# Spacing the block chains of a fused four-layer graph network: transposes and weight products one stage further behind, last block's factors from two banks

## The chip, the cores and the metric

The kernel runs on one core of a Trainium2 chip. The metric is the device time of one execution in microseconds; before the change it is 2231.47 us (median of 3 runs, 2231.07 to 2232.33). The profile is one execution of the same kernel with a span of 2227.8 us.

A core has five engines with one instruction queue each: PE (TensorE, matrix products and transposes), DVE (VectorE), ACT (ScalarE), POOL (GpSimd) and SP (SyncE, which issues the loads). They meet through semaphores. PE writes into PSUM banks, from which DVE and ACT read.

## The reference, cut to what matters

Four graph layers over 4096 nodes with 128 features each, one dense 4096x4096 matrix `adj` (64 MB in float32), and after each layer a residual and a layer norm:

```python
# layer 0: signed attention;  layer 1: two Chebyshev convolutions with elu
x = _layernorm(x + _L0_gnn_ref(x, adj, adj, W, a))
x = _layernorm(x + _L1_gnn_ref(x, adj, W0, b0, W1, b1))
# layer 2: 4 heads of 32, dense attention with multiplicative adj
h_prime = (x @ weight.T).reshape(n, heads, f_out)
C = alpha_src[None, :, :] + alpha_dst[:, None, :]
tau = adj_t * exp(maximum(0.2 * C, C))
z = einsum('mnh,nhf->mhf', adj_t * tau / tau.sum(axis=1, keepdims=True), h_prime)
x = _layernorm(x + z + bias)
# layer 3: h @ W_self + (adj @ h / clip(adj.sum(1), 1)) @ W_neigh
x = _layernorm(x + _L3_gnn_ref(x, adj, W_self, W_neigh))
```

For layer 2 the kernel splits the exponential into factors of the source node (`es`, `cs`, and `hc`, the head's features times `cs`) and of the target node (`dv`, from which `D` is spread over the partitions), so that a weight is `max(D, es) * a`.

## The kernel before, in words

Nodes are taken in blocks of 512 (`IB`; 8 blocks, `NB`) and tiles of 128 (32 tiles, `NT`; four of them, `TB`, per block). Layer 1 ends in a product of the adjacency with `w`, block by block: 32 loop products (L1104) of 128x512 per block add up in one bank, `pp` (block 1 in `num`). When a block is done, its chain of small steps ends layer 1 for it and prepares layer 2:

- `block_end` (L741): DVE adds and applies the elu (L748 to L752, with ACT's L750 and L751) into `oT`; PE transposes it (L754); DVE adds it to `x` and takes the statistics (L756 to L763), ACT normalizes (L766); PE transposes `x` (L768); ACT copies the result to `xT` (L770), POOL adds a bias row (L772); then two halves of the weight product (L778, `W2S`), each followed by two exponentials on ACT (`cs` and `es`, L780 and L781) and two products on DVE (`hc`, L784).
- `block_targets` (L788): PE's product with `WD` (L792), an exponential and a split into three bf16 parts on ACT and DVE (L794 to L801).
- `targets` of the first two passes (L841): PE's product with `selD` (L851), copied to `D` by ACT (L854).

All PE steps of the chain, other than a second product of some `targets`, write one bank, `px` (pool `ps_x` with one buffer), so that each waits for the reader of the one before. In the trace the two kinds of transposes show as L137, the line of their helper.

Layer 2 itself is a row of passes over all 32 tiles (class `Pass`). One `step` (L857) makes the weights of one tile: DVE computes `tau` (L866, twice 128x1024) and the first 704 columns of `tau2` (L872), POOL the rest of it (L873, L874). `tau` comes in four buffers. `load` (L818) has ACT copy the adjacency tile to a PSUM bank `a` and sum it (L838); passes 0 and 1 share a tile, so there is a copy for every two steps. `product` (L883) has PE add `tau` to `den` and `tau2` to `num`, four matrix products of 32 rows each, called a row of products here.

The order on PE, DVE, ACT and POOL is written out by hand (`manual_schedule`): an instruction stands in its engine's queue in the order in which the Python code emits it. Chains are generators in the queue `chains`, and `one(chains)` takes the first of them to its next `yield`. So a `yield` is a turn: what follows is emitted behind the loop products of the next turn. For the first three blocks the turn comes after every two loop products; from block 3 on (`ib > 2`) steps of passes 0 and 1 are mixed in, and the turn comes after two or four loop products, twice for each segment of `cuts` (L1094), with a `products()` at each segment's end. A block's chain thus runs in the loop of the next block. The chain of the last block runs in the `while` loop of L1123, where `held` says that this chain is not done; there an iteration has two steps and two rounds of `one(chains)` or more, and no loop products of layer 1. The remaining passes of layer 2 and layer 3's product with the adjacency (L977) follow, mixed as well.

Of the kernel before, what the change touches and what calls it, by code (L numbers as in the profile page):

```python
# [11 lines left out]
F32 = mybir.dt.float32  # L12
BF16 = mybir.dt.bfloat16
I32 = mybir.dt.int32
AF = mybir.ActivationFunctionType
# [4 lines left out]
P = 128  # L20
IB = 512
TB = IB // P
# [11 lines left out]
def adj_resnorm_d4(ctx: ExitStack, tc: tile.TileContext, x_in, xT_in, adj, adjT, w0g, w0gT, a0, w1a, b1a,  # L34
# [7 lines left out]
    nc = tc.nc  # L42
    N, F = x_in.shape
    NT = N // P
    NB = N // IB
# [3 lines left out]
    H = att_src.shape[1]  # L49
    FO = F // H  # L50
# [31 lines left out]
    es = const.tile([P, NT, H], F32, name="es")  # L82
    cs = const.tile([P, NT, H], F32, name="cs")
# [49 lines left out]
    def transpose4(pool, name, src, order=lambda r: r):  # L133

        p = pool.tile([P, TB, P], F32, name=name)
        for k in range(TB):
            order(nc.tensor.transpose(p[:, k, :], src(k), ident))  # L137
        return p
# [486 lines left out]
    def network(usual):  # L625

        with ExitStack() as whole:
# [113 lines left out]
            def block_end(ib, p):  # L741

                blk = slice(ib * IB, (ib + 1) * IB)
                tb = slice(ib * TB, (ib + 1) * TB)
                oT = l2w.tile([P, IB], F32, name="oT", tag="z")
                rn = l2w.tile([P, 2, IB], F32, name="rn", tag="nd")
                r, n = rn[:, 0, :], rn[:, 1, :]
                nc.vector.tensor_add(oT, p, h0T[:, blk])  # L748
                nc.vector.tensor_scalar(n, oT, B1B, 0.0, op0=ALU.add, op1=ALU.min)
                nc.scalar.activation(n, n, AF.Exp)  # L750
                nc.scalar.activation(r, oT, AF.Relu, bias=B1B)  # L751
                nc.vector.scalar_tensor_tensor(oT, n, -1.0, r, op0=ALU.add, op1=ALU.add)  # L752
                yield
                q = transpose4(ps_x, "px", lambda k: oT[:, k * P:(k + 1) * P])  # L754
                yield
                nc.vector.tensor_add(x[:, tb, :], q, x[:, tb, :])  # L756
                for t in range(ib * TB, (ib + 1) * TB):
                    stats(x[:, t, :], t)
                s = small.tile([P, TB], F32, name="rstd")
                m = small.tile([P, TB], F32, name="mean")  # L760
                nc.scalar.activation(s, mv[:, tb, 1], AF.Sqrt, bias=eps)
                nc.vector.reciprocal(s, s)
                nc.vector.scalar_tensor_tensor(m, mv[:, tb, 0], -1.0, s, op0=ALU.mult, op1=ALU.mult)  # L763
                for k in range(TB):
                    r = x[:, ib * TB + k, :]
                    nc.scalar.activation(r, r, AF.Identity, bias=m[:, k:k + 1], scale=s[:, k:k + 1])  # L766
                yield
                q = transpose4(ps_x, "px", lambda k: x[:, ib * TB + k, :])  # L768
                yield
                nc.scalar.copy(xT[:, blk], q.rearrange("p k i -> p (k i)"))  # L770
                nc.scalar.activation(m[:, 0:1], m[:, 0:1], AF.Exp, scale=0.0)
                nc.gpsimd.tensor_tensor(x[:, tb, :], x[:, tb, :], B2R[:, None, :].to_broadcast([P, TB, F]), ALU.add)  # L772
                for half in range(2):
                    two = slice(ib * TB + 2 * half, ib * TB + 2 * half + 2)
                    pn = ps_x.tile([P, 2, F + H], F32, name="px")
                    for k in range(2):
                        t = ib * TB + 2 * half + k
                        nc.tensor.matmul(pn[:, k, :], xT[:, t * P:(t + 1) * P], W2S, start=True, stop=True)  # L778
                    yield
                    nc.scalar.activation(cs[:, two, :], pn[:, :, F:F + H], AF.Exp, scale=0.2)  # L780
                    nc.scalar.activation(es[:, two, :], pn[:, :, F:F + H], AF.Exp, scale=0.8)  # L781
                    for k in range(2):
                        t = ib * TB + 2 * half + k
                        nc.vector.tensor_mul(hc[:, t], pn[:, k, 0:F].rearrange("p (h f) -> p h f", f=FO),  # L784
                                             cs[:, t, :][:, :, None].to_broadcast([P, H, FO]))
                ended.append(ib)

            def block_targets(ib):  # L788

                blk = slice(ib * IB, (ib + 1) * IB)  # L790
                pd = ps_x.tile([96, IB], F32, name="px")
                nc.tensor.matmul(pd, WD, xT[:, blk], start=True, stop=True)  # L792
                yield
                nc.scalar.activation(pd, pd, AF.Exp, scale=-0.8)  # L794
                nc.scalar.copy(dv[:, blk], pd)
                yield
                nc.vector.tensor_sub(pd, pd, dv[:, blk])
                nc.scalar.copy(dv[32:64, blk], pd[32:64, :])
                nc.scalar.copy(dv[64:96, blk], pd[64:96, :])
                nc.vector.tensor_sub(pd[64:96, :], pd[64:96, :], dv[64:96, blk])  # L800
                nc.scalar.copy(dv[64:96, blk], pd[64:96, :])  # L801

            def weights(nt, head, den):
                return cs[:, nt, head:head + 1].to_broadcast([P, FO]) if den else hc[:, nt, head, :]

            class Pass:
# [50 lines left out]
                def step(self, nt, a, ap):  # L857

                    assert self.made == 4
                    tau = l2w.tile([P, 4, IB], F32, name="tau", bufs=4)  # L860
                    tau2 = l2w.tile([P, 4, IB], F32, name="tau2", bufs=4)
                    n = 2 if self.wide else 1
                    flat = lambda t: t.rearrange("p q i -> p (q i)")
                    for q in range(0, 4, n):
                        head = self.parts[q][0]
                        nc.vector.scalar_tensor_tensor(flat(tau[:, q:q + n]), flat(self.D[:, q:q + n]),  # L866
                                                       es[:, nt, head:head + 1], ap, op0=ALU.max, op1=ALU.mult)
                    if self.wide:
                        t, t2 = flat(tau), flat(tau2)

                        only = self is passes[1] and layer1_done
                        nc.vector.tensor_tensor(t2[:, 0:OWN], t[:, 0:OWN], (a if only else ap)[:, 0:OWN], ALU.mult)  # L872
                        nc.gpsimd.tensor_tensor(t2[:, OWN:WB], t[:, OWN:WB], a[:, OWN:WB], ALU.mult)  # L873
                        nc.gpsimd.tensor_tensor(t2[:, WB:2 * WB], t[:, WB:2 * WB], a, ALU.mult)  # L874
                    else:
                        own = OWN4 // 2
                        rep = lambda v, q: v[:, None, :].to_broadcast([P, q, v.shape[1]])
                        nc.vector.tensor_tensor(tau2[:, 0:2, 0:own], tau[:, 0:2, 0:own], rep(ap[:, 0:own], 2), ALU.mult)  # L878
                        nc.gpsimd.tensor_tensor(tau2[:, 0:2, own:IB], tau[:, 0:2, own:IB], rep(a[:, own:IB], 2), ALU.mult)  # L879
                        nc.gpsimd.tensor_tensor(tau2[:, 2:4, :], tau[:, 2:4, :], rep(a, 2), ALU.mult)  # L880
                    return tau, tau2
# [140 lines left out]
            with tc.manual_schedule(engines={mybir.EngineType.PE, mybir.EngineType.DVE, mybir.EngineType.Activation,  # L1022
# [100 lines left out]
                while todo:  # L1123
                    step()
                    if wait:
                        wait = bool(pieces) and not one(pieces)
                    held = NB - 1 not in ended
                    if not held:
                        load()
                    if todo[0] == (passes[1], NT - 1):  # L1130
                        while passes[2].made < 4:
                            one(chains)
                    one(chains)
                    if held:
                        load()
                    step()
                    if not pieces:
                        one(chains)
                    load()
                    products()  # L1140
                    one(chains)
                    credit = min(credit + (2.0 if todo and todo[0][0].wide else 3.4), 6.0) if pieces else 0.0
                    while credit >= 1.0 and pieces and not wait:
                        credit -= 1.0
                        wait = one(pieces)
# [48 lines left out]
```

## Time and profile before

| | |
|---|---|
| time | 2231.47 us (2231.07 to 2232.33, 3 runs) |
| span of the profile | 2227.8 us, 22992 instructions |
| PE | 2135.1 us busy (96%) |
| DVE | 1184.2 us (53%) |
| POOL | 857.6 us (38%) |
| ACT | 562.5 us (25%) |
| DMA | 528.18 MB, mean 237 GB/s |
| granted PE clock, mean | 0.988 |

Times in the profile are microseconds from the start of the span, unless marked ns. A row of the view in order of time gives the start, the duration, the engine, the line and operation, what is written and read, the number of instructions merged, and in brackets the idle time of the engine before it and what ended that. A float32 matrix product shows as two records. Ends on PE are modelled, so rows overlap a little; starts are what to subtract. A row of waits gives total us, times and the longest. A row of stretches gives the stretch and its length, then for each engine its busy us (and instructions), then PE's granted clock, the DMA share and GB/s.

### The profile page before, as it was taken

Reading aid. Unit: us, or ns where it says so; the run is one execution under the profiler, and the core shown is the slowest. Engines: PE = TensorE matmul, PEld = TensorE weight load, DVE = VectorE, ACT = ScalarE, POOL = GpSimd, SP = SyncE. Lnnn points to the kernel's source line nnn. Section 1 sums busy time; section 2 is a strip of 40 time slices with the busy share of each in tenths; the row PEclk is TensorE's granted clock in tenths of the full one; section 3 lists DMA queues with packets and bytes.
Section 4 is the critical chain, followed back from the end, with each engine's and each line's share of the span. In section 5 each row is a group of like instructions: output and inputs, shape, how many; then the busy total and the mean of one; then the engine's idle time right before and its main releaser. Section 6 shows DMA issues by size and latency. Waiting matters only on the chain. (4 is left out here: it accounts for less than half of the span.)

```text
span 2227.8 us, 22992 instructions
## 1 busy us (share of the span) xinstructions
PE 2135.1 (96%) x8644; PEld 847.9 (38%) x8644; DVE 1184.2 (53%) x1832; ACT 562.5 (25%) x1014; POOL 857.6 (38%) x539
## 2 busy tenths in 40 slices
PE   8999999999999999999999999978999899999997
PEld 4344454444444444444443333322222222233333
DVE  5655460000011110000016787789999999999995
ACT  6755010000000000000033223235333433332213
POOL 0000000000000000000004776688999899989980
PEclk9999999999999999999999999989999999999999
DMA  9886658888767768777867556524666566635554
GB/s 396 333 324 228 224 196 288 301 300 301 268 231 253 245 226 279 262 261 262 280 235 248 187 196 224 208 76 170 240 234 243 189 246 241 225 135 194 189 173 170
DMA packets 87145, 528.18 MB, mean 237 GB/s; under 512 B 9328, under 2 KB 15472, under 8 KB 25712
## 3 DMA queue, kind: packets, MB, share of 16 engines
q1 hardware_dynamic: 80288, 521.64, 66.6%
q10 hardware_dynamic: 6736, 4.98, 0.7%
q8 instruction: 70, 1.15, 0.2%
q14 instruction: 51, 0.42, 0.1%
HBM read 524.49 MB, written 2.10 MB: 236 GB/s over the span
## 5 line engine op out<-in xcount | busy, mean ns | idle before, releaser
L866 DVE SCALAR_TENSOR_TENSOR tau<-D,es,a 128x1024 f32<-128x1024 f32 (+1 forms) x640 | 647.0, 1061 | 52.5 <-ACT a L838 32.0
L874 POOL TENSOR_TENSOR tau<-tau,chunk 128x1024 f32<-128x1024 f32 x192 | 459.4, 2392 | 12.3 <-DVE tau L866 11.7
L772 POOL TENSOR_TENSOR x<-x,B2R 128x512 f32<-128x512 f32 x8 | 10.2, 1274 | 1148.0 <-PE px L137 1148.0
L890 PE MATMUL num<-tau,hc 128*32 128x512 f32 x2048 | 331.5, 612 | 13.2 <-POOL tau L874 6.7
L890 PE MATMUL den<-tau,cs 128*32 128x512 f32 x2048 | 336.0, 602 | 2.1 <-DVE tau L866 0.4
L977 PE MATMUL pp<-chunk,xT 128*128 128x512 f32 (+1 forms) x488 | 231.7, 604 | 0.0
L838 ACT ACTIVATE a<-chunk 128x1024 f32<-128x1024 f32 x160 | 164.3, 1027 | 249.9 <-DVE tau L872 193.4
L664 PE MATMUL pacc<-chunk,t 128*128 128x512 f32 x512 | 223.5, 592 | 0.0
L664 PE MATMUL pacc<-chunk,v 128*128 128x512 f32 x512 | 222.5, 592 | 0.0
L664 PE MATMUL pacc<-chunk,x 128*128 128x512 f32 x512 | 222.1, 592 | 0.0
L873 POOL TENSOR_TENSOR tau<-tau,chunk 128x320 f32<-128x320 f32 x192 | 168.0, 875 | 133.6 <-DVE tau L866 74.0
L1104 PE MATMUL pp<-chunk,w 128*128 128x512 f32 x448 | 203.5, 598 | 0.8 <-DVE oT L748 0.8
L379 PE MATMUL pacc<-chunk,hw 128*128 128x512 f32 x408 | 187.1, 603 | 1.1 <-DVE numT L407 1.1
L872 DVE TENSOR_TENSOR tau<-tau,a 128x704 f32<-128x704 f32 x186 | 163.6, 880 | 0.0
L880 POOL TENSOR_TENSOR tau<-tau,chunk 128x1024 f32<-128x1024 f32 x64 | 152.2, 2377 | 1.0
L890 PEld LDWEIGHTS num<-tau,hc 128*32 128x32 f32 x2048 | 61.2, 110 | 231.0 <-issue 125.5
L890 PEld LDWEIGHTS den<-tau,cs 128*32 128x32 f32 x2048 | 79.0, 111 | 173.7 <-issue 98.7
L664 PEld LDWEIGHTS pacc<-chunk,v 128*128 128x128 f32 x512 | 97.2, 190 | 122.0 <-issue 122.0
L664 PEld LDWEIGHTS pacc<-chunk,x 128*128 128x128 f32 x512 | 96.3, 190 | 115.8 <-issue 115.8
L664 PEld LDWEIGHTS pacc<-chunk,t 128*128 128x128 f32 x512 | 96.1, 190 | 115.3 <-issue 115.3
L977 PEld LDWEIGHTS pp<-chunk,xT 128*128 128x128 f32 x488 | 85.7, 190 | 128.6 <-issue 125.8
L711 DVE COPY w<-ptr 128x512 f32<-128x512 f32 x8 | 5.5, 692 | 241.5 <-PE ptr L137 241.5
(238 smaller groups left out, 1688.1 us busy)
## 6 DMA issues: line engine op xcount, KB each, us to landing
chunk<-in_adjT SPq DMA_DIRECT2D x386, 1024.0 KB, 4.9
chunk<-in_adj SPq DMA_DIRECT2D x80, 1024.0 KB, 5.0
chunk<-in_adj SPq DMA_DIRECT2D x32, 512.0 KB, 5.1
keep<-in_adjT SPq DMA_DIRECT2D x13, 1024.0 KB, 10.8
xT<-in_xT ACTq DMA_DIRECT2D x8, 256.0 KB, 6.5
out<-o ACTq DMA_DIRECT2D x7, 256.0 KB, 2.3
W1A<-in_w1a ACTq DMA_DIRECT2D x1, 384.0 KB, 5.6
W1B<-in_w1b ACTq DMA_DIRECT2D x1, 384.0 KB, 7.5
```

The costliest lines, as they stand in the source:

```text
L379: in_order(nc.tensor.matmul(p, hw[:, j * TB + k, :], a[:, k, :], start=first and k == 0, stop=last and k == TB - 1))
L664: nc.tensor.matmul(p, stationary(c * TB + k), a[:, k, :], start=n == 0 and k == 0, stop=n == NB - 1 and k == TB - 1)
L772: nc.gpsimd.tensor_tensor(x[:, tb, :], x[:, tb, :], B2R[:, None, :].to_broadcast([P, TB, F]), ALU.add)
L838: nc.scalar.activation(ap, a, AF.Copy, accum_out=deg[:, nt, self.mp:self.mp + 1])
L866: nc.vector.scalar_tensor_tensor(flat(tau[:, q:q + n]), flat(self.D[:, q:q + n]), es[:, nt, head:head + 1], ap, op0=ALU.max, op1=ALU.mult)
L872: nc.vector.tensor_tensor(t2[:, 0:OWN], t[:, 0:OWN], (a if only else ap)[:, 0:OWN], ALU.mult)
L873: nc.gpsimd.tensor_tensor(t2[:, OWN:WB], t[:, OWN:WB], a[:, OWN:WB], ALU.mult)
L874: nc.gpsimd.tensor_tensor(t2[:, WB:2 * WB], t[:, WB:2 * WB], a, ALU.mult)
L880: nc.gpsimd.tensor_tensor(tau2[:, 2:4, :], tau[:, 2:4, :], rep(a, 2), ALU.mult)
L890: nc.tensor.matmul(acc[32 * q:32 * q + 32, :], weights(nt, head, is_den), r[:, q, :], start=nt == 0, stop=nt == NT - 1)
L977: nc.tensor.matmul(p, y[:, c * TB + k, :], a[:, k, lo:lo + n], start=c == blocks[0] and k == 0, stop=end)
L1104: nc.tensor.matmul(p, w[:, c * TB + k, :], a[:, k, :], start=c == 0 and k == 0, stop=c == NB - 1 and k == TB - 1)
```

## The change

It adds `yield`s to the chains, so that some of their PE steps stand behind more of other work, and rearranges the last block:

- Blocks 0 to 2: one turn more ahead of the transposes of `oT`.
- Blocks 0 to 5: one turn more between the copy of `xT` and the first half of the weight product.
- Blocks 0 and 1: one turn more at the end of `block_targets`, ahead of the products with `selD`.
- Last block: both halves of the weight product are emitted together, the second into the bank `pp`, and the exponentials and `hc` of both follow.
- While the last chain is not done, the copy of the next tile (`load`) is emitted right after the second step, ahead of the turn of the chain, instead of behind it.

The purpose is that PE should not stand before a chain step whose input is still being made. No instruction is added or taken away. The diff, with the loop's new lines cut only where they repeat the old ones with a further indent:

```diff
@@ block_end
+                pns = []
                 oT = l2w.tile([P, IB], F32, name="oT", tag="z")
...
                 nc.vector.scalar_tensor_tensor(oT, n, -1.0, r, op0=ALU.add, op1=ALU.add)
                 yield
+                if ib <= 2:
+                    yield
                 q = transpose4(ps_x, "px", lambda k: oT[:, k * P:(k + 1) * P])
...
                 nc.gpsimd.tensor_tensor(x[:, tb, :], x[:, tb, :], B2R[:, None, :].to_broadcast([P, TB, F]), ALU.add)
+                if ib < NB - 2:
+                    yield
                 for half in range(2):
-                    two = slice(ib * TB + 2 * half, ib * TB + 2 * half + 2)
-                    pn = ps_x.tile([P, 2, F + H], F32, name="px")
+                    pool, name = (ps_p, "pp") if ib == NB - 1 and half else (ps_x, "px")
+                    pn = pool.tile([P, 2, F + H], F32, name=name)
                     for k in range(2):
                         t = ib * TB + 2 * half + k
                         nc.tensor.matmul(pn[:, k, :], xT[:, t * P:(t + 1) * P], W2S, start=True, stop=True)
+                    pns.append(pn)
+                    if ib == NB - 1 and half == 0:
+                        continue
                     yield
-                    nc.scalar.activation(cs[:, two, :], pn[:, :, F:F + H], AF.Exp, scale=0.2)
...
+                    for pn, at in zip(pns, range(half + 1 - len(pns), half + 1)):
+                        two = slice(ib * TB + 2 * at, ib * TB + 2 * at + 2)
+                        nc.scalar.activation(cs[:, two, :], pn[:, :, F:F + H], AF.Exp, scale=0.2)
...
+                    pns.clear()
                 ended.append(ib)
@@ block_targets
                 nc.scalar.copy(dv[64:96, blk], pd[64:96, :])
+                if ib < 2:
+                    yield
@@ the loop after layer 1
                     if held:
                         load()
                     step()
+                    if held:
+                        load()
                     if not pieces:
                         one(chains)
-                    load()
+                    if not held:
+                        load()
                     products()
```

More of the change, by code (lines that the diff above doesn't have):

```diff
@@ L778, in block_end @@
                         nc.tensor.matmul(pn[:, k, :], xT[:, t * P:(t + 1) * P], W2S, start=True, stop=True)
+                    pns.append(pn)
+                    if ib == NB - 1 and half == 0:
+                        continue
                     yield
-                    nc.scalar.activation(cs[:, two, :], pn[:, :, F:F + H], AF.Exp, scale=0.2)
[L781 to L785, printed above, removed]
+                    for pn, at in zip(pns, range(half + 1 - len(pns), half + 1)):
+                        two = slice(ib * TB + 2 * at, ib * TB + 2 * at + 2)
+                        nc.scalar.activation(cs[:, two, :], pn[:, :, F:F + H], AF.Exp, scale=0.2)
+                        nc.scalar.activation(es[:, two, :], pn[:, :, F:F + H], AF.Exp, scale=0.8)
+                        for k in range(2):
+                            t = ib * TB + 2 * at + k
+                            nc.vector.tensor_mul(hc[:, t], pn[:, k, 0:F].rearrange("p (h f) -> p h f", f=FO),
+                                                 cs[:, t, :][:, :, None].to_broadcast([P, H, FO]))
+                    pns.clear()
                 ended.append(ib)
```

## The prediction

> **What bounds the kernel now.** The page of the profile comes first: PE is busy for 2135.1 of 2227.8 us (96%), DVE for 53%, POOL for 38%. The slices show that PE reads 9 nearly everywhere and dips once, at slices 26 and 27 of 40 (7, then 8), so at 1448 to 1504 us; DVE is at 5 to 9 from slice 21 on. The chain of waits is no help here: its listed pieces begin at 1681 us. So I read stretches. The changed code runs from 1105.55 to about 1460 us; each row below is the product loop of one block (blocks 1 to 7), the last row what follows it.
>
> ```profile
> core 0: us, PE busy (x) PEld busy (x) DVE busy (x) ACT busy (x) POOL busy (x), PEclk, DMA share, GB/s
> 1105.55:1141.15 35.60, 32.24 (x87) 14.46 (x86) 6.83 (x20) 12.26 (x24) 1.26 (x1) 1.00 0.68 237
> 1141.15:1177.55 36.40, 32.40 (x88) 14.28 (x86) 7.55 (x22) 12.26 (x24) 1.26 (x1) 1.00 0.71 241
> 1177.55:1223.30 45.75, 44.73 (x203) 17.60 (x203) 33.52 (x46) 16.29 (x32) 26.88 (x17) 1.00 0.67 233
> 1223.30:1280.87 57.57, 55.13 (x278) 19.49 (x274) 45.38 (x56) 16.35 (x33) 39.70 (x25) 1.00 0.55 195
> 1280.87:1338.55 57.68, 55.14 (x279) 19.50 (x275) 45.37 (x56) 16.46 (x34) 39.74 (x25) 1.00 0.56 201
> 1338.55:1388.69 50.14, 49.15 (x247) 18.51 (x243) 38.82 (x50) 15.41 (x32) 33.33 (x21) 1.00 0.64 231
> 1388.69:1438.73 50.04, 49.16 (x247) 18.51 (x243) 38.82 (x50) 15.32 (x31) 33.33 (x21) 1.00 0.59 203
> 1438.73:1460.66 21.93, 11.12 (x56) 4.19 (x56) 16.69 (x28) 7.93 (x18) 14.71 (x9) 0.73 0.19 78
> ```
>
> Up to 1438.73 PE is the bound: all else idles for 10 us or more per block, and the DMA share is at most 0.71. In the last row PE works half the time at clock 0.73, and DVE is the busiest. Who PE waits for in this stretch:
>
> ```profile
> PE px L778 <- DVE hc L784: 8.7, 4, 5.6
> PE px L137 <- ACT x L766: 5.4, 5, 3.3
> PE px L137 <- DVE oT L752: 3.3, 2, 1.7
> PE px L851 <- ACT dv L801: 2.2, 2, 1.1
> PE px L792 <- DVE hc L784: 1.9, 2, 1.0
> PE num L890 <- POOL tau L874: 1.8, 3, 0.6
> ```
>
> These are the waits that the change aims at (total us, times, longest). Two views in order of time, PE and then DVE, show the last block:
>
> ```profile
> 1449.05 1.63 PE L137 MATMUL px<-ident,x 128*128 128x128 f32 x4 [3.27 <-ACT x L766]
> 1451.85 1.25 PE L778 MATMUL px<-W2S,xT 128*128 128x132 f32 x4 [1.18 <-ACT xT L770]
> 1458.72 1.22 PE L778 MATMUL px<-W2S,xT 128*128 128x132 f32 x4 [5.62 <-DVE hc L784]
> ```
>
> ```profile
> 1448.30 0.16 DVE L763 SCALAR_TENSOR_TENSOR mean<-mv,rstd 128x4 f32<-128x4 f32 x1
> 1451.29 2.47 DVE L866 SCALAR_TENSOR_TENSOR tau<-D,es,a 128x1024 f32<-128x1024 f32 x2 [2.83 <-ACT a L838]
> ...
> 1460.25 0.49 DVE L784 TENSOR_TENSOR hc<-px,cs 128x128 f32<-128x128 f32 x2 [1.68 <-ACT es L781]
> 1460.66 1.27 DVE L866 SCALAR_TENSOR_TENSOR tau<-D,es,a 128x1024 f32<-128x1024 f32 x1
> ```
>
> **What the Trainium skill says.** (1) "PSUM — Partial Sum Buffer", section on bank collisions: an engine must not touch a bank while another one does, so access is guarded by bank. The trace agrees: all chain steps share the one bank px, and the second weight product stands 5.62 us until DVE has read the first. (2) "TensorE: Matmul & The Clock Gate", on queue depths: ACT and DVE are strict FIFO. The trace agrees: the copy a (1450.06) starts behind the four normalizations of ACT's queue, and DVE stands 2.83 us for it. (3) The same page, Part 1: an idle PE falls to half clock. Here after 5.62 us idle the next eight num records take 1.71 us from start to start, where 0.86 is usual.
>
> **The change part by part.** Prices from PE's order in time: two loop products take 1.72 us (four records), four 3.43, eight 6.97 with the turn; four weight transposes 0.43 to 0.49, a half weight product 0.45, WD 0.87, one row of num and den products 1.72, two rows 3.44. On DVE a tau step (two L866, one L872) takes 3.19.
>
> *Blocks 0 and 1* run between loop products alone. Transposes of oT now come after four products instead of two: the waits of 1.73 and 1.59 fall within the added 1.72, saving 1.7 and 1.6. D's first product (L851) comes after six instead of four: waits 1.11 and 1.11 fall within 1.72. Transposes of x still come four products behind oT's, so their waits stay. Sum: -2.8 and -2.7, **-5.5**. The yield ahead of the weight products hides nothing here; these didn't wait.
>
> *Block 2* (45.75 us). The second weight product moves past a round of two rows and no longer meets hc: -1.02. But transposes of x come one turn later, and DVE now has a third tau step queued ahead of L756: L756 starts at 1186.73 + 1.27 (copy a, as at 1200.36) + 3.19 = 1191.2. In the trace the four transposes run from 3.74 to 5.06 us after L756 starts, so they end at 1196.25; PE arrives at 1194.73 and would end at 1195.2. That is +1.06. Sum **0.0**.
>
> *Block 3* (57.57 us) is the cost. Block 2's WD product now is the last chain step of its loop, so its targets (L794 to L801) run in the next loop, in the turn that ends with oT's transposes of block 3. These write px and must wait for L801. Queued ahead of L797 on DVE are L748 to L752 and two tau steps. From the start S of the loop: WD ends about 3.5 before S and L748 starts at S-4.4; L752 at +2.53; tau 1.10 behind; two steps 6.38; so L797 starts at S+5.6; from L797's start to L801's end the trace has 3.24 (1214.98 to 1218.22): S+8.9. PE arrives at S+3.5: a new wait of **5.4**. Behind it on PE stand two rows and all loop products; DVE needs none of them at once, since the tau buffer of its next step is free already, so DVE goes on. In return the waits of before in this loop fall: DVE catches up meanwhile, so POOL's delay (rows at 1237.15 to 1242.63 take 5.48 instead of 3.5) goes, -2.0, and hc, -1.03. x's transposes wait as before (1.5 before, 1.3 by the same sum). From S the end of the second round comes at +21.7, before at +19.3; the half weight product that was inside it, 0.5, follows; hc's 1.03 is saved: +1.9. Half clock after 5.4 idle would add 1.6 as after 5.62 (0.4 on the transposes, 0.85 and 0.35 on rows), of which the wait of x's transposes hides 1.2: +0.4. Sum **+2.3**; bounds -1 (targets done in time) and +4.5 (nothing won back).
>
> *Blocks 4 and 5* (57.68 and 50.14). Block 4: POOL's wait ends when POOL does (1298.42), so the weight product taken out of its shadow costs 0.45, the second waits 0.4 instead of 1.01: **-0.3**. Block 5: WD no longer meets hc: **-1.0**. Block 6 keeps its order, 0.
>
> *Block 7.* The next tile's copy now stands ahead of the square root and normalizations on ACT: the tau step follows L763 at 1448.46 rather than 1451.29, -2.83. Both weight products go out together, into px and pp, right behind x's transposes; PE's 5.62 goes. But from here DVE sets the pace (DVE 28.68 and POOL 30.00 of 30 us at 1470 to 1500, PE 24.40), so only DVE's own loss counts: its 1.68 for es at the second half. The next copy (L838) now precedes cs and es on ACT and ends at about 1455.4, es at 1455.6, DVE's hc starts at 1455.7 instead of 1454.9: 0.8 lost there, but the tau step at 1460.66 finds its copy ready and starts at 1456.6. Sum **-4.1**; bounds 0 (another engine takes over) and -6.1 (what PE alone would gain). pp is free, its last reader being L748 at 1435.26.
>
> The instruction counts stay. Past 1460 us the order on all engines is the old one, and DVE, POOL and PE are busy for 91 to 100 of every 100 us up to 2100, so I carry the shift to the end one for one.
>
> Total: -5.5 + 0.0 + 2.3 - 0.3 - 1.0 + 0 - 4.1 = **-8.6**; 2231.47 - 8.6 = **2222.9 us**.
>
> **Rivals.** *The targets end in time* (ACT and DVE ahead of my sum): block 3 then saves all its 1.53 + 2.0 + 1.03 = 4.6, total -5.5 - 4.6 - 0.3 - 1.0 - 4.1 = -15.5, 2216.0 us. Against it: DVE's FIFO puts 6.38 us of tau ahead of L797.
> *The last block pays nothing*, as POOL, with 30.00 of 30 us busy later, takes over: -4.5, 2227.0 us. For it: POOL's steps take 3.25 to 3.9; against: POOL stands 5.11 and 0.81 us within 1440 to 1462, waiting for DVE.
> *The waits are only passed on* (slower): block 2 +1.06 and block 3 +5.4 + 1.6 + 1.3, nothing won back, blocks 4 to 7 zero, and of blocks 0 and 1 only the 3.3 at oT: +9.4 - 3.3 = +6.1, 2237.6 us. Against it: POOL's delay comes of DVE lagging, and a standing PE lets DVE catch up.
>
> **How the numbers follow.** My sum 0.67, targets in time 0.10, last block nothing 0.17, passed on 0.06. Faster by over 0.2% is below 2227.0: all of the first two and a third of the third, 0.83; the rest of it, 0.11, is within; slower 0.06. The range cuts the extreme cases: 2218.0 (4.9 below, most of the way to the first rival) to 2228.5 (block 3 at +4.5 and the last block at -0.7, which is +5.6).
>
> **What would show it.** Right: no wait for oT or L801 in the loops of blocks 0 and 1, each shorter by 2.7; a wait of about 5 us of px transposes for ACT's dv copy near 1222 us, that loop near 60 us; no POOL wait in it; the tau step straight behind L763 in the last block, 5.62 gone. Wrong: that wait absent or far longer; DVE or POOL standing after 1450 for something new; a later stretch that takes back the lead.

## The result, and the profile after

The changed kernel takes **2222.75 us** (median of 4 runs, 2222.57 to 2223.48) against 2231.9 us (4 runs, 2231.07 to 2233.1) for the kernel before: ratio 0.9959, 95% interval 0.9942 to 0.9976. The forecast was 2222.9 us, faster. In a later set the same kernel took 2224.47 us (5 runs, 2219.86 to 2224.92) against 2231.09, ratio 0.9966 (0.9952 to 0.998): the gain is 6.6 to 9.2 us, and the closeness of 2222.9 is partly luck.

The profiled run has a span of 2221.7 us, with PE busy for 2136.2 us (2135.1 before) and DVE for 1186.1 (1184.2). So hardly any work was added or taken away; the gain lies in when engines stand. The view of stretches is divided as before at the loops of blocks 1 to 7, and its last row runs from the end of the last loop to the fifth tau step behind it. The loop of a block runs the chain of the block before it. As in the prediction, "block 3" means from here on the chain of block 3 with the loop that it runs in, the fourth row, and "block 7" the last row:

```profile
core 0: us, PE busy (x) PEld busy (x) DVE busy (x) ACT busy (x) POOL busy (x), PEclk, DMA share, GB/s
1105.50:1138.10 32.60, 32.07 (x87) 14.47 (x86) 6.83 (x20) 12.26 (x24) 1.27 (x1) 1.00 0.74 261
1138.10:1171.51 33.41, 32.12 (x87) 14.29 (x85) 7.54 (x22) 12.26 (x24) 1.27 (x1) 1.00 0.76 258
1171.51:1216.93 45.42, 45.18 (x202) 17.74 (x202) 32.90 (x45) 14.45 (x29) 26.94 (x17) 1.00 0.69 244
1216.93:1277.03 60.10, 54.71 (x278) 20.10 (x274) 46.07 (x58) 18.51 (x36) 39.67 (x25) 0.94 0.51 178
1277.03:1334.35 57.32, 55.58 (x278) 19.50 (x274) 45.61 (x56) 15.97 (x32) 39.79 (x25) 1.00 0.56 201
1334.35:1385.06 50.71, 49.19 (x246) 18.51 (x243) 39.25 (x51) 15.94 (x32) 33.38 (x21) 1.00 0.65 230
1385.06:1435.10 50.04, 49.16 (x246) 18.51 (x243) 38.82 (x50) 15.31 (x31) 33.29 (x21) 1.00 0.58 203
1435.10:1452.55 17.45, 12.77 (x72) 4.77 (x72) 16.61 (x27) 7.92 (x18) 13.14 (x9) 0.80 0.23 97
```

Row by row against before: -3.00, -2.99, -0.33, **+2.53**, -0.36, **+0.57**, 0.00, **-4.48**; the sum is -8.06. Two rows grew. The waits of PE in 1095 to 1500 us name what stands where:

```profile
PE px L137 <- ACT dv L813: 5.4, 1, 5.4
PE px L137 <- ACT x L769: 4.6, 4, 3.3
PE px L784 <- DVE hc L795: 1.8, 2, 1.5
PE px L804 <- DVE hc L795: 0.9, 1, 0.9
PE num L904 <- POOL tau L888: 8.2, 9, 1.2
```

The waits for DVE's `oT` ahead of the transposes (3.3 us before) and for `dv` ahead of D's first product (2.2) are gone, and hc's fell from 8.7 to 1.8. The waits for POOL's part of `tau` grew from 4.7 to 8.2 us in this window; 7.0 of them lie behind 1453 us, where DVE and POOL set the pace and PE waits for them. New is one wait of 5.4 us for `dv`. In order of time on PE it stands in block 3's loop, and what follows it runs at half clock (1.71 and 1.36 us from start to start, then 0.86):

```profile
1226.02 1.12 PE L137 MATMUL px<-ident,oT 128*128 128x128 f32 x4 [5.39 <-ACT dv L813]
1227.07 1.94 PE L904 MATMUL num<-tau,hc 128*32 128x512 f32 x8
1228.78 1.54 PE L904 MATMUL den<-tau,cs 128*32 128x512 f32 x8
1230.14 1.03 PE L904 MATMUL num<-tau,hc 128*32 128x512 f32 x8
1231.00 1.03 PE L904 MATMUL den<-tau,cs 128*32 128x512 f32 x8
```

The last block, PE and then DVE in order of time:

```profile
1445.42 1.63 PE L137 MATMUL px<-ident,x 128*128 128x128 f32 x4 [3.26 <-ACT x L769]
1447.72 1.25 PE L784 MATMUL px<-W2S,xT 128*128 128x132 f32 x4 [0.68 <-ACT xT L773]
1448.76 1.09 PE L784 MATMUL pp<-W2S,xT 128*128 128x132 f32 x4
```

```profile
1444.67 0.16 DVE L766 SCALAR_TENSOR_TENSOR mean<-mv,rstd 128x4 f32<-128x4 f32 x1
1444.75 2.47 DVE L880 SCALAR_TENSOR_TENSOR tau<-D,es,a 128x1024 f32<-128x1024 f32 x2
...
1451.75 0.49 DVE L795 TENSOR_TENSOR hc<-px,cs 128x128 f32<-128x128 f32 x2
1452.15 0.48 DVE L795 TENSOR_TENSOR hc<-pp,cs 128x128 f32<-128x128 f32 x2
1452.55 2.46 DVE L880 SCALAR_TENSOR_TENSOR tau<-D,es,a 128x1024 f32<-128x1024 f32 x2
```

DVE goes from L766 straight into the tau step, reads both banks one after the other, and shows no idle time between 1444.67 and 1452.55. PE's 5.62 is gone; its 3.26 for x stays.

### The profile page after: what moved, and what is told of

Same layout as the page of the kernel before. It is cut to its first block, busy times and chain, and to the rows that moved or that the text cites. A ratio compares the mean times of both kernels' runs of the same rounds, so it can differ in the third digit from the quotient of the medians.

```text
span 2221.7 us, 23001 instructions
## 1 busy us (share of the span) xinstructions
PE 2136.2 (96%) x8644; PEld 847.9 (38%) x8644; DVE 1186.1 (53%) x1832; ACT 562.8 (25%) x1014; POOL 857.5 (39%) x539
```

## The experiments

Each is an edit of the kernel before or of the changed kernel. Two things are read from each trace besides the time: the distances between DVE's adds into `oT` (L748 before, L749 after), which mark the loops in which the chains of blocks 0 to 6 run, and the last stretch, with block 7's chain, from the last such add to the first reciprocal of a pass. The adds stand close to the loop starts but not on them, so these distances differ from the stretches above by up to 3.6 us in the middle blocks (41.84 for 45.42 in block 2).

| kernel | time, us (range, runs) | ratio to before (95%) | distances, chains of blocks 0 to 6 | last |
|---|---|---|---|---|
| before | 2231.9 (2231.07-2233.1, 4) | | 35.52 35.45 43.03 57.58 57.67 50.15 50.03 | 56.28 |
| changed | 2222.75 (2222.57-2223.48, 4) | 0.9959 (0.9942-0.9976) | 32.53 32.47 41.84 60.96 57.32 50.71 50.04 | 51.80 |
| changed, again | 2224.47 (2219.86-2224.92, 5) | 0.9966 (0.9952-0.998) | 32.53 32.46 41.84 61.32 57.31 50.70 50.03 | 51.80 |
| last block's edits alone | 2225.86 (2224.48-2226.64, 10) | 0.9975 (0.9965-0.9984) | 35.52 35.46 43.02 57.56 57.65 50.13 50.03 | 51.80 |
| added turns alone | 2227.89 (2224.57-2229.5, 13) | 0.9978 (0.997-0.9987) | 32.53 32.46 41.84 61.67 57.31 50.70 50.03 | 56.27 |
| copy ahead alone | 2228.78 (2226.07-2230.8, 18) | 0.999 (0.9982-0.9997) | as before | 53.57 |
| second bank alone | 2229.58 (2228.15-2231.87, 10) | 0.9991 (0.9981-1.0001) | as before | 54.70 |
| without block 2's turns | 2219.97 (2218.56-2221.63, 4) | 0.9948 (0.9932-0.9965) | 32.54 32.46 43.03 57.30 57.90 50.71 50.03 | 51.78 |
| without the turn of the targets | 2225.53 (2224.81-2227.8, 7) | 0.9977 (0.9965-0.9989) | 33.81 33.74 41.84 61.38 57.33 50.72 50.04 | 51.82 |
| without block 5's turn | 2226.15 (2223.34-2228.42, 7) | 0.9981 (0.9969-0.9993) | 32.54 32.46 41.85 60.54 57.32 50.65 50.03 | 51.79 |
| turns re-placed | 2218.94 (2215.65-2219.22, 4) | 0.9939 (0.9923-0.9956) | 31.14 31.08 43.02 57.30 57.92 49.33 49.55 | 52.60 |
| min on ACT | 2224.43 (2221.54-2228.08, 18) | 0.997 (0.9963-0.9977) | 32.75 32.70 42.07 62.37 57.54 50.35 50.26 | 52.01 |
| re-placed, min on ACT | 2218.38 (2218.09-2218.67, 2) | 0.9943 (0.9923-0.9962) | 31.38 31.31 43.25 57.54 57.54 48.98 48.97 | 52.00 |
| re-placed, min on ACT from block 3 on | **2216.14** (2215.87-2217.31, 4) | 0.9935 (0.9919-0.9952) | 31.15 31.08 43.02 57.55 57.55 48.99 49.34 | 53.04 |

The kernel before, run beside each group, had medians of 2230.22 to 2231.9 us. The times of one kernel spread by up to 6.5 us (before: 2228.93 to 2235.41 in one group), the distances of loops that an edit leaves alone repeat to some 0.1 us (only block 3's, behind the half clock, moves more: 60.54 to 61.67 with block 2's turns in and the DVE form of the min). So the parts are read from the distances.

### The two halves of the change

Last block's edits alone, relative to the changed kernel (the three added turns taken out):

```diff
-                if ib <= 2:
-                    yield
...
-                if ib < NB - 2:
-                    yield
...
-                if ib < 2:
-                    yield
```

> The kernel before with the two edits of the last block alone (second half of the weight product in the bank pp, next tile's copy ahead of the turn); no added turn in any block. Theory A (parts add up): the loops of blocks 1 to 7 keep their lengths of before (35.6, 36.4, 45.8, 57.6, 57.7, 50.1, 50.0 us), and the stretch from the last loop's end to the fifth tau step behind it is 4.5 us shorter (17.4 instead of 21.9), so the time is 4 to 4.5 us below before, about 2227.4. Theory B (the last block pays nothing because POOL or PE takes over behind it): the lead of 4.5 us is gone again by 1600 us, time as before. Theory C (all the gain is the last block's): 9 us below before.

Added turns alone (the load and the banks as before):

```diff
-                    pool, name = (ps_p, "pp") if ib == NB - 1 and half else (ps_x, "px")
+                    pool, name = (ps_x, "px")
...
-                    if ib == NB - 1 and half == 0:
-                        continue
...
-                    if held:
-                        load()
...
-                    if not held:
-                        load()
+                    load()
```

> The changed kernel with its added turns, but the last block as before. Theory A: the loops as in the changed kernel (32.6, 33.4, 45.4, 60.1, 57.3, 50.7, 50.0 us, together 3.6 us less than before), the last block as before (21.9 us to the fifth tau step), so 3.6 us below before, about 2228.0. Theory B: the whole gain, 8 to 9 us. Theory C: no gain, since the waits in the loops are only passed on.

The two don't interact: with the last block's edits alone all loops stay as before and the last stretch has the changed kernel's 51.80; with the turns alone the loops are the changed kernel's and the last stretch is the old 56.27. In the distances the first is worth 4.5 us and the second 3.6 (the seven distances add up to 329.43 before, 325.87 after; 2.9 in the trace of the turns alone, where block 3 took 61.67); their sum is the 8.0 of both. In time they were worth 5.5 and 3.5 against the 2231.35 us (22 runs) of the kernel before measured beside them.

### The two edits of the last block

Copy ahead alone, relative to the kernel before:

```diff
                     step()
+                    if held:
+                        load()
                     if not pieces:
                         one(chains)
-                    load()
+                    if not held:
+                        load()
```

> The kernel before with the copy of the next tile emitted ahead of the last chain's turn, and nothing else: one px bank, no new turns. Loops of blocks 0 to 6 as before. Read: the stretch from DVE's last add into oT to the first reciprocal of a pass (before 56.28, after 51.80). Theory A (the copy and the bank save separate waits of DVE, 2.83 and 1.68 less 0.4 lost): the tau step starts straight behind L763's, the PE wait of about 5.6 for hc stays, stretch 53.4 to 53.8, time 2228 to 2229. Rival B (the second half through the one bank is what sets the end, an earlier tau step only stands in front of it on DVE): the PE wait grows, stretch 56 or more, time as before.

Second bank alone, relative to the kernel before:

```diff
-                    pn = ps_x.tile([P, 2, F + H], F32, name="px")
+                    pool, name = (ps_p, "pp") if ib == NB - 1 and half else (ps_x, "px")
+                    pn = pool.tile([P, 2, F + H], F32, name=name)
...
+                    if ib == NB - 1 and half == 0:
+                        continue
                     yield
```

> The kernel before with both halves of the last weight product emitted together, the second into pp, and nothing else: the copy stays behind the turn. Read: the same stretch (before 56.28, after 51.80). Theory A: DVE still stands 2.8 us for the copy a, PE's 5.62 for hc is gone, DVE's 1.68 for es is gone: stretch 54.4 to 54.8, time about 2230. Rival B: the bank is the whole gain, stretch about 51.8 to 52.5. Rival C: the bank alone is worth nothing while DVE stands for the copy, stretch 56 or more.

Copy ahead: -2.71; second bank: -1.58; together 4.29 of the 4.48. In time the copy's gain is barely clear of the noise and the bank's isn't (0.9981 to 1.0001); only the distances tell them apart. Theory A of both held in its sizes: two separate waits of DVE, each removed by its own edit. DVE with the copy ahead and one bank:

```profile
1448.59 0.16 DVE L764 SCALAR_TENSOR_TENSOR mean<-mv,rstd 128x4 f32<-128x4 f32 x1
1448.67 2.47 DVE L872 SCALAR_TENSOR_TENSOR tau<-D,es,a 128x1024 f32<-128x1024 f32 x2
...
1455.66 0.49 DVE L789 TENSOR_TENSOR hc<-px,cs 128x128 f32<-128x128 f32 x2
1457.83 0.49 DVE L789 TENSOR_TENSOR hc<-px,cs 128x128 f32<-128x128 f32 x2 [1.68 <-ACT es L786]
```

The 2.83 is gone and the 1.68 stays to the digit. With the bank alone it is the reverse: 2.82 stays, 1.68 goes. A detail of the first expectation failed: PE's wait for hc, which was to stay at 5.6, fell to 3.41, since DVE comes to hc earlier. With the bank alone PE's 5.62 is gone altogether, and the stretch is still only 1.58 shorter, about DVE's 1.68. So DVE sets the end of this stretch.

### Block 2's turns, which cost block 3

```diff
-                if ib <= 2:
+                if ib < 2:
                     yield
...
-                if ib < NB - 2:
+                if ib < NB - 2 and ib != 2:
                     yield
```

> The changed kernel without the two added turns of block 2, whose target factors then are done within its own loop. Theory A (block 2's turns push its targets into the next loop, where the transposes of oT stand 5.39 us for them): that wait is gone, block 2's loop is 45.7 us and block 3's 57.2 instead of 60.1, 2.6 us in all, about 2220.2. Rival (the 5.4 us are time that DVE needs anyhow in block 3's loop, so PE stands later instead): the wait comes back as longer waits for POOL and for the normalization in the same loop, the loop stays near 60 us, and the time is that of the changed kernel, 2222.8.

Block 3's distance falls from 60.96 to 57.30 and block 2's rises from 41.84 to 43.03: both return to before's within 0.3. All seven distances together are 1.9 us shorter than the changed kernel's; the time is 2.8 us lower, part of which lies far behind ("The stretch far behind"). So these two turns were a loss: they make block 2's target factors late for block 3's transposes, which write the same bank. Block 4's distance is 57.90 instead of 57.32; why is seen below, at DVE's L750.

### The turn of the targets

```diff
-                if ib < 2:
-                    yield
```

> The changed kernel without the one turn at the end of the target factors (blocks 0 and 1). Theory A (each turn saves the wait in front of its own product): waits of 1.1 for dv in front of D's first product come back in both loops, 32.53 and 32.47 become 33.6 each, all other loops the same, time 1 to 3 us over that of the changed kernel. Rival B (the turn ahead of the transposes already moves the whole chain back far enough): loops stay at 32.5.

The waits come back at D's first product, 1.11 us in both loops, and the distances rise by 1.28 and 1.27. Theory A held: this turn pays for the wait ahead of its own product.

### The turns re-placed

```diff
-                if ib <= 2:
+                if ib < 2:
                     yield
                 q = transpose4(ps_x, "px", lambda k: oT[:, k * P:(k + 1) * P])
...
+                if ib < 2:
+                    yield
                 q = transpose4(ps_x, "px", lambda k: x[:, ib * TB + k, :])
...
-                if ib < NB - 2:
+                if ib in (3, 4):
                     yield
...
+                if ib in (NB - 3, NB - 2):
+                    yield
                 pd = ps_x.tile([96, IB], F32, name="px")
```

> As the one without block 2's turns, and the turns set where waits were seen: in blocks 0 and 1 the turn ahead of the weight product moves ahead of the transposes of x (these stand 1.2 us each in both kernels); block 5 loses the turn ahead of its weight product; blocks 5 and 6 get one ahead of the product with WD. Theory A, from 2220.2: loops of blocks 1 and 2 1.2 us shorter each (31.4 and 32.2), block 5's loop back from 50.7 to 49.2, block 6's from 50.0 to 49.2: 2.4 + 1.5 + 0.9 = 4.8 us less, about 2215.4. Rival (each turn moves a wait to the next step of the chain): loops as in the one without block 2's turns, 2220.2.

Against the kernel without block 2's turns, blocks 0 and 1 ("loops of blocks 1 and 2" in the expectation) fall by 1.4 each (x's transposes had stood 0.34 and then taken 1.48 us, in pieces, behind ACT's normalizations), block 5 by 1.4 and block 6 by 0.5. The last stretch grew by 0.8, and the time fell by 1.0 alone, where the distances together give 3.8. The next two parts take up both misses.

### Why block 5's loop grew

The turn ahead of block 5's weight product was to save the 0.99 us ahead of WD. It was taken out by itself:

```diff
-                if ib < NB - 2:
+                if ib < NB - 3:
                     yield
```

> The changed kernel without the added turn ahead of block 5's weight product; blocks 0 to 4 keep theirs. Theory A (in the loop of block 5's chain the turn moves the second half of the weight product to where hc stands behind two tau steps of DVE, 1.52 us, and in return saves 0.99 ahead of WD): without it the wait of 1.5 goes, the wait of 1.0 ahead of WD returns, that loop is 50.1 instead of 50.71, loop of the next block 50.04. Rival B (50.71 comes from the turn of block 3 and 4 before it, DVE lagging): that loop stays at 50.7.

Theory A failed: the loop stayed at 50.65, against 50.71 with the turn. The number is the rival's. With the turn, PE and DVE in the changed kernel show

```profile
1358.32 0.61 PE L784 MATMUL px<-W2S,xT 128*128 128x132 f32 x4
1358.77 1.88 PE L1118 MATMUL pp<-chunk,w 128*128 128x512 f32 x4
1362.18 0.69 PE L784 MATMUL px<-W2S,xT 128*128 128x132 f32 x4 [1.52 <-DVE hc L795]
```

```profile
1355.18 2.47 DVE L880 SCALAR_TENSOR_TENSOR tau<-D,es,a 128x1024 f32<-128x1024 f32 x2 [1.27 <-issue]
1357.57 0.88 DVE L886 TENSOR_TENSOR tau<-tau,a 128x704 f32<-128x704 f32 x1
1358.37 2.47 DVE L880 SCALAR_TENSOR_TENSOR tau<-D,es,a 128x1024 f32<-128x1024 f32 x2
1360.75 0.88 DVE L886 TENSOR_TENSOR tau<-tau,a 128x704 f32<-128x704 f32 x1
1361.55 0.48 DVE L795 TENSOR_TENSOR hc<-px,cs 128x128 f32<-128x128 f32 x2
```

hc stands behind a second whole tau step of DVE's queue, and two loop products don't cover that. Without the turn the wait is at WD instead:

```profile
1361.62 1.07 PE L804 MATMUL px<-xT,WD 128*96 128x512 f32 x2 [1.17 <-DVE hc L795]
```

So the turn only moves the wait. What is left, 0.5 us over before in both, is DVE being late by as much from the beginning of the loop. From its add to its first `hc` DVE takes 27.00 us before and 30.66 in the changed kernel; one more tau step, 3.19, and 0.49 for one operation that takes 1.08 us instead of 0.59 make up that difference. This operation, before and after, and POOL's beside it:

```profile
1335.81 0.59 DVE L749 TENSOR_SCALAR rn<-oT,B1B 128x512 f32<-128x512 f32 x1
```

```profile
1333.74 2.37 POOL L874 TENSOR_TENSOR tau<-tau,chunk 128x1024 f32<-128x1024 f32 x1
```

```profile
1331.62 1.08 DVE L750 TENSOR_SCALAR rn<-oT,B1B 128x512 f32<-128x512 f32 x1
```

```profile
1330.04 2.38 POOL L888 TENSOR_TENSOR tau<-tau,chunk 128x1024 f32<-128x1024 f32 x1
```

The same operation takes 0.49 us where POOL is idle. Here it ends 0.29 us after POOL's step in the first pair (1336.40 against 1336.11) and 0.28 after it in the second (1332.70 against 1332.42). The Trainium skill, "SBUF — State Buffer", section "Who interferes with whom", says that a `tensor_scalar` in DVE's two-port mode and a GpSimd operation exclude each other for a whole instruction, the later one blocking; the durations agree, with 0.3 us behind it. In all eleven traces that have the eight of these operations on DVE, where a POOL step ends 0.3 us or more behind the operation's start, the operation ends 0.28 or 0.29 us behind that step; the others take 0.48 or 0.49 us. The kernel without block 2's turns has 1.08 in block 4's chain too, and its block 4 is 0.58 longer than the changed kernel's, where that operation took 0.49; the re-placed one has 1.31 in its last chain, and PE waits 0.65 for `oT` there.

To test it, DVE's operation was moved to ACT, as relu(-v), then exp of its negative:

```diff
+            nc.vector.tensor_scalar(NB1B, B1B, -1.0, None, op0=ALU.mult)
...
-                nc.vector.tensor_scalar(n, oT, B1B, 0.0, op0=ALU.add, op1=ALU.min)
-                nc.scalar.activation(n, n, AF.Exp)
+                nc.scalar.activation(n, oT, AF.Relu, bias=NB1B, scale=-1.0)
+                nc.scalar.activation(n, n, AF.Exp, scale=-1.0)
```

> The changed kernel with min(v, 0) ahead of the elu's exponential computed on ACT as relu(-v), exp(-that), in place of DVE's L750. It tells what made block 5's loop 50.71 us long. In the changed kernel L750 took 1.08 us in that chain instead of 0.49, and ended 0.28 us after POOL's step that had begun before it. Theory A (DVE stands for POOL's step there and its whole queue of that loop is late for it): with no such operation on DVE, DVE's first hc of that chain comes 0.5 to 1.0 us earlier after the add into oT (30.66 in the changed kernel), PE's wait for it falls from 1.52 to 0.5 to 1.0, and that loop takes 49.7 to 50.2. Rival B (the 1.08 is hidden by DVE's later wait for ACT or for the copy a, which end it anyway): hc stays at about 30.7 and the loop at 50.7, or longer as ACT has 0.6 us more in the chain. Other loops within 0.5 of the changed kernel's.

hc starts 30.30 us after the add instead of 30.66, PE's wait is 1.17 instead of 1.52, the loop 50.35 instead of 50.71. That is neither theory's size: the direction is A's, but the longer chain on ACT takes part of it back (the second add into `oT` comes at +2.76; +3.12 with the blocked operation, +2.63 in the kernel before). In the other loops, block 3's apart, nothing was blocked and the move costs 0.2: PE now stands 0.2 longer for `oT`. With this cost added back the move is worth 0.36 + 0.22 = 0.58 in block 5, as much as the 0.59 by which the blocked operation is longer than 0.49.

The same on the re-placed turns, and then for the chains of blocks 3 to 7 alone (`if ib < 3` keeps the DVE form):

> The re-placed turns of e4_respaced with the same move of L750 to ACT. Theory A: in the last two chains of e4_respaced L750 took 1.30 and 1.31 us beside POOL's step; without it PE's wait of 0.65 for oT in the last stretch goes, and the stretch from the last add into oT to the first reciprocal is 51.6 to 52.0 instead of 52.60; loops of blocks 5 and 6 stay at 49.3 and fall to 49.1 to 49.5. Time 2215 to 2220, the fastest so far. Rival B (ACT's extra 0.6 us lengthens the last chain): stretch 52.6 or more.

> The turns of e4_respaced, with min(v, 0) on ACT for the chains of blocks 3 to 7 alone, those that run beside POOL's steps; the first three chains stay as in e4_respaced. Theory (the move helps only where DVE stood for POOL, and costs 0.2 where it did not): loops 31.1, 31.1, 43.0 as in e4_respaced, 57.5, 57.5, 49.0, 49.0 as in e10_respaced_act, last stretch 52.0: 1.0 to 1.5 us below both up to the first reciprocal, time 2216.5 to 2218. Rival (the 0.2 in the first loops came of something else): loops as in e10_respaced_act, time 2218 or more.

With the move everywhere, blocks 5 and 6 fall below what was expected, to 48.98 and 48.97, and the last stretch to 52.00 as expected; the first loops pay 0.2 each. Kept to blocks 3 to 7 it gives the first loops back (31.15, 31.08, 43.02) and the lowest median of all, 2216.14 us, with all four times under those of the kernel before and of the changed kernel. The expected sum was missed: block 6 took 49.34 and the last stretch 53.04, so the first reciprocal came no earlier than in the other two, 1.0 us later in fact (1478.07 against 1477.07). PE keeps a lead of 0.42 us over the kernel with the move everywhere to the end of block 6's loop, but DVE comes to its add at 1425.03, against 1425.07: its queue is the bound by then. The 1.0 us is the clock's. DVE's queue is the same in both to within 0.05 us up to 1476; then the reciprocal stands 0.94 us for PE's transposes, as PE had half clock for 6.83 us from 1469.72 on, and for 3.41 from 1470.67 on in the other. The lower time comes from far behind, as the next part shows, so that this kernel is better than the other two re-placed ones isn't shown.

### The stretch far behind

The lead of the changed kernel's trace is a steady 8.1 to 8.2 us at every reciprocal from 1491 to 1938 us of before's time, and 6.4 at the next, 2060: the distance from the sixth to the seventh is 122.77 before and 124.58 after. PE in order of time there, before and after:

```profile
1965.28 1.94 PE L890 MATMUL num<-tau,hc 128*32 128x512 f32 x8
1966.99 1.27 PE L890 MATMUL den<-tau,cs 128*32 128x512 f32 x8
```

```profile
1965.26 1.94 PE L904 MATMUL num<-tau,hc 128*32 128x512 f32 x8
1966.96 1.93 PE L904 MATMUL den<-tau,cs 128*32 128x512 f32 x8
1968.67 1.94 PE L904 MATMUL num<-tau,hc 128*32 128x512 f32 x8
```

Three rows at half clock in a run where before has one. The clock that PE was granted there (PEclk), before and then after:

```profile
core 0: us, PE busy (x), PEclk, DMA share, GB/s
1960.62:1964.03 3.41, 1.50 (x9) 1.00 0.31 92
1964.04:1967.45 3.41, 3.41 (x16) 0.50 0.57 215
1960.23:1963.64 3.41, 1.13 (x4) 1.00 0.00 0
1963.65:1967.06 3.41, 2.32 (x13) 0.50 0.00 0
1967.06:1970.47 3.41, 3.41 (x24) 0.50 0.02 5
```

In all fourteen traces the time at half clock between the two reciprocals goes with the distance:

| at half clock, us | distance from sixth to seventh reciprocal, us | kernels |
|---|---|---|
| 3.41 | 122.73 to 122.79 | before, copy alone, bank alone, without block 2's turns, without the targets' turn, re-placed with ACT from block 3 |
| 6.83 | 124.45 to 124.58 | changed (both traces), last block alone, turns alone, without block 5's turn, min on ACT |
| 10.24 | 126.19 to 126.20 | re-placed, re-placed with min on ACT |

The order of the instructions in this stretch is the same in all. One run, of the changed kernel unaltered, asked whether it belongs to the kernel or to the run:

> The changed kernel once more, unaltered. Read: the time from the sixth to the seventh reciprocal of the passes, far behind the changed code: 124.58 in the changed kernel's trace, 122.77 before; the other kernels so far showed 122.7 to 122.8 or 124.5 to 124.6, but for one of 126.2. Theory A (a matter of the phase of PE's clock in the single run): this trace may show the other value, and the times of this kernel spread over 2 us or more. Rival B (a property of the order): 124.5 again, and times within 1 us.

The second trace of the changed kernel again shows 124.45 and 6.83 us at half clock, as Theory B said; but its five times spread from 2219.86 to 2224.92, as Theory A said, with clocks from 0.987 to 0.990. By themselves these two traces don't settle the question.

The granted clock on record in the traces tells more. Between 70 and 2150 us half clock comes in stretches of 3.41 us or of two, three or four times that, and in each trace all of these begin on one grid of 3.41 us. The grid isn't tied to the program: its first point lies 0.99 us behind the start of the span in one trace of the changed kernel and 1.77 in the other. Where the sixth reciprocal stands behind a point of the grid sorts the three lengths without an exception: 0.29 to 1.26 us gives 122.7, 1.81 or 1.83 gives 126.2, and 3.34 to 3.41 or 0.16 to 0.24 gives 124.5. So the length goes with the phase, as Theory A has it, and each 3.41 us more at half clock cost 1.7, its half. Whether the phase at that place is chance or follows in part from the order further ahead stays open: both traces of the changed kernel got the same length. The longer stretch takes back 1.8 of the changed kernel's 8.2 us and 3.4 of the re-placed one's gain in their traces. The Trainium skill, "TensorE: Matmul & The Clock Gate", Part 1, has the clock follow a free-running window of activity of some 3.4 us; the grid of 3.41 us agrees.

The traces also show how much work keeps the clock up. Of their 8389 windows of the grid at full clock, 92 were followed by one at half clock. In these 92 PE was busy for at most 1.63 of the 3.41 us; of the other 8297, all but ten had more. (PE's ends are modelled, so the border is rough.) So a wait need not be long: before, two waits of 1.23 and 0.68 us fell into one window, which left 1.50 us of work. In the changed kernel the same two fell on both sides of a point of the grid and cost no clock, but a later one of 2.22 us did, which left 1.13 us of work.

## Why the prediction held, and where not

- *Blocks 0 and 1*, predicted -2.8 and -2.7: -3.00 and -2.99, with no wait left for `oT` or `dv`. Right, and the run without the targets' turn puts 1.3 of each on that turn (1.1 predicted).
- *Block 2*, predicted 0.0: -0.33. The wait of 1.06 us for x, which was to eat the gain, came: it shows not as idle time but as a longer row of x's transposes, before and after:

```profile
1191.30 0.65 PE L137 MATMUL px<-ident,x 128*128 128x128 f32 x4
1188.92 1.49 PE L137 MATMUL px<-ident,x 128*128 128x128 f32 x4
```

From the row's start to that of the next it is 0.49 and 1.42 us, so 0.93 of the 1.06. hc's 1.02 is gone, as said. The remaining 0.2 was not taken further.
- *Block 3*, predicted +2.3 with a new wait of 5.4: +2.53 with 5.39. Right to the size, by the queue on DVE ahead of the targets. The wait for x, kept at 1.3 in the sum, is absent in the trace, as the half clock made PE late: it cost 0.5 us on the transposes and 1.3 on the four rows shown (4.89 from 1227.07 to 1231.96, where the next four take 3.57), 1.8 for the 1.6 of the sum. DVE didn't simply go on: it stood 1.84 us, up to 1227.19. The rival that had the targets end in time is refuted; so is the one that passed all waits on.
- *Block 4*, predicted -0.3: -0.36.
- *Block 5*, predicted -1.0: +0.57. **This step failed.** It said "WD no longer meets hc", which is true, and took that for the saving. The wait went to the second half of the weight product, 1.52 us, as hc now stands behind two tau steps: the turn by itself costs 0.06 (50.71 against 50.65 without it). The other 0.5 is DVE's `tensor_scalar` behind POOL's step, 1.08 us instead of 0.59, for the whole queue of that loop, a term that the prediction didn't have; the move to ACT took 0.36 of it back, after its own cost of 0.2.
- *Block 6*, predicted 0: 0.00.
- *Block 7*, predicted -4.1: -4.48, by the steps given: 2.71 by the copy alone and 1.58 by the bank alone, for 2.83 and 1.68 in the prediction; of the 0.4 that it took off for hc starting later nearly nothing is seen. The rival that the last block pays nothing is refuted by its own run, 2225.86 us with these edits alone.
- *Carried to the end one for one*: right to 1938 us; behind that the clock takes 1.8 us in the profiled pair, whose spans differ by 6.1. So one sign of being wrong, a later stretch that takes back the lead, came true in part. That the medians of the first set are 9.2 apart, so close to the sum, is in part luck: in the later set it is 6.6.

The sum was off by 0.5 us at the end of the stretches: predicted -8.6, measured -8.06. Block 5's miss of 1.6 was made good by 1.0, of which 0.5 came in blocks 0 and 1, 0.3 in block 2, and 0.4 in block 7, less 0.2 in block 3.

## What to carry to other kernels

A later place in one queue helps only if the reader's own queue has come that far: count what stands ahead of the reader on its engine in the very loop in question, since one more tau step of 3.2 us undid a turn here. Before a turn is spread over all blocks, look for the last chain step that still fits into its loop, as one that falls over the edge meets the next chain's first step on the same bank (5.39 us), and try the turns block by block. Look at DVE's durations too, and not only at its idle time: an operation that is blocked shows there as a longer one. Where the times spread more than the parts are worth, read the parts from distances between marks in the traces, which repeat to 0.1 us.

## What the runs showed of the hardware

- A `TENSOR_SCALAR` of 128x512 on DVE takes 0.49 us alone, and 0.59, 1.08, or 1.31 when a POOL step that began before it ends 0.3, 0.8, or 1.0 us after its start. So a changed order in one chain can shift the whole loop of another block by half a microsecond.
- PE's half clock came in units of 3.41 us on a grid of its own, which stood elsewhere in each execution. It followed windows in which PE was busy for less than about 1.6 of 3.41 us, by waits as short as 1.23 and 0.68 us together.
- Programs with the same order of instructions in a stretch took 122.7, 124.5, or 126.2 us for it, with 3.41, 6.83, or 10.24 us at half clock, by where the grid stood.
